# Two-layer transformer sandwich, fp32: in the attention steps the value matmuls go ahead of all the step's row-maximum scores

## The chip, the core and the metric

One Trainium2 chip; the kernel runs on one of its cores. The metric is device time of one execution in microseconds (us). The kernel before takes 1508.69 us, the median of three executions (1508.69 to 1511.38).

Names in the profile: PE is TensorE (matmuls), PEld its weight loads, DVE is VectorE, ACT is ScalarE, POOL is GpSimd, SP is SyncE, which here only issues DMAs. "L725" is line 725 of the kernel. A group such as `ex<-psc,mask` names the tile written and the tiles read.

## The reference

Activations `x` are 2 batches x 1024 tokens x 512, fp32. Four blocks, each of the form x = x + layernorm(block(layernorm(x))):

1. a grouped-query block in which each head's softmax runs over one score,
2. a feed-forward block with ternary weights (512 to 1408 to 512),
3. causal attention with rotary position embedding, 16 heads of width 32, 4 key/value groups (four heads to a group), 1024 tokens,
4. a feed-forward block (512 to 2048 to 512) with 2:4 sparsity of the hidden values.

The change lies in block 3, which computes

```
q = x @ q_w.T ; k, v = split(x @ kv_w.T)      # q, k rotated
logits = q @ k.T / sqrt(32) + causal mask
probs  = softmax(logits)
out    = (probs @ v) @ c_w.T
```

## The kernel before, in words

**Tiling of the attention.** A task is one batch, one block Q of 512 queries (two per batch) and one key/value group with its four heads: 2 x 2 x 4 = 16 tasks. Keys come in tiles of 128. With Q = 0 a task looks at 4 key tiles, with Q = 1 at 8.

**Scores are computed twice.** The softmax needs each row's maximum and sum first, and the probabilities with keys on the partitions afterwards.

- The *row-maximum scores* (`score_step`, tile `psc`, L725) have 128 queries on the partitions and up to 512 keys in the free dimension. For each PSUM tile DVE adds the mask, writes the negated scores to SBUF (`ex`) and takes the running minimum (L736); for Q = 1 a head's row has two such chunks, and the second takes the first's result (`mx`) as its start. Then ACT runs the exponential over the row with its sum (L742, `ex<-ex,mxs`).
- When a task's scores are done, some 20 small DVE instructions compute minus the logarithm of the sum plus the maximum (`minus_log`, L184, tiles `lg*`), split it into three bf16 pieces (`pm`), and PE transposes these (L955) to `mT`. The small DVE instructions are kept in a list and dropped, two after each score pass, into DVE's order (`drip`).
- The *key-side scores* (`prob_step`, tile `pst`, L1021) have 128 keys on the partitions and 512 queries in the free dimension, one matmul for each of the four heads; a bf16 *shift matmul* for each head (L1028) adds `mT` to them in PSUM. ACT then takes the exponential (L1034), which is the finished probability `pT`. On the diagonal POOL sets the masked part to zero (L1036), and tiles there are narrower: 512, 384, 256, 128.
- The *values* (`value_step`, tile `po`, L1050) multiply `pT` by `v`: eight matmul instructions (fp32 in two passes for four heads), 32 output columns each.

**Order.** PE and POOL run in the order in which the code issues them; DVE is so ordered only where the code says so (score passes and small drops), and otherwise DVE and ACT are ordered by the compiler's scheduler. The main loop (L1301) makes 96 steps, one for each key tile of each task. In step s: key-side scores and shifts of tile s, then row-maximum scores of a *later* task, then the values of tile s-1, whose exponentials have run meanwhile, then whatever is due in this step (projections `pq`, `pkv` of the next batch, output products `py` of a finished one, transposes). `wanted` (L1210) says how many row-maximum steps must be done by then, at a rate of 4/3 for each step, so a step has none, one (4 matmuls) or two (8).

The values are not put ahead of or behind all of these scores but after the first half of the first row-maximum step: `scores_up_to` calls `between` after the first group of heads, and `between` runs the values once. If a step has no scores, the values come directly after the shifts.

**PSUM.** Eight banks. Key-side scores and row-maximum scores share a ring of seven (`ring`: tags `a` with four and `o` with three, in turn), so each new tile needs the bank of the tile seven before it, emptied by ACT (`pst`) or DVE (`psc`). Values accumulate in the eighth (`ps_v`). `ex` has three buffers, `pT` four (two to a step).

```
L1198  for n_h, heads in enumerate(hs):
L1199      score_step(tk, ii, heads, ring)
L1200      if n_h == 0:
L1201          between()
...
L1307  waiting = [lambda: values(step)]
...
L1314  scores_up_to(wanted(step), step, between)
L1315  between()
```

Of the kernel before, what the change touches and what calls it, by code (L numbers as in the profile page):

```python
# [24 lines left out]
def two_layer_sandwich(  # L25
# [175 lines left out]
    def in_order(f):  # L201
        with tc.manual_schedule(engines={mybir.EngineType.DVE}):
            f()

    def drip(n, idle=False, upto=None):


        while n > 0 or (upto is not None and len(shift_drops.items) > upto):
            q = shift_drops if shift_drops.items else norm_drops
            if not q.items:  # L210
                return
            f, cost = q.items.pop(0)
            n -= cost
            if f is not None:
                f()
            elif idle:
                while q.items and q.items[0][0] is None:
                    q.items.pop(0)
                return
# [363 lines left out]
    def flush():  # L583
        while waiting_adds:
            waiting_adds.pop(0)()
# [121 lines left out]
    def score_sums(tk, pool):  # L707
        tk.mx = pool.tile([P, GT, REP], F32, tag="mxs", name=f"mxs_{tk.nm}", bufs=3)
        tk.sm = pool.tile([P, GT, REP], F32, tag="sms", name=f"sms_{tk.nm}", bufs=3)

    def score_step(tk, ii, heads, bank):


        n = GW * tk.Q + (ii + 1) * P
        for r in heads:
            ex = None
            if tk.n > 0:
                ex = s1.tile([P, NQ * GW], F32, tag="ex", name=f"ex_{tk.nm}_{ii}_{r}", bufs=3)
            mx = tk.mx[:, ii, r : r + 1]
            least = 3.0e38  # L720
            for ch in range(tk.Q + 1):
                k0 = ch * GW
                w = min(GW, n - k0)
                pa = bank(f"psc_{tk.nm}_{ii}_{ch}_{r}")
                nc.tensor.matmul(  # L725
                    pa[:, :w], tk.q.bitcast(F32R)[:, r, ii * P : (ii + 1) * P],
                    tk.st.k[ch].bitcast(F32R)[:, tk.g, :w], start=True, stop=True,
                )
                to, m0 = mx, GW + P - w
                if ch < tk.Q:  # L730
                    to = s1.tile([P, 1], F32, tag="mx1", name=f"mx1_{tk.nm}_{ii}_{r}", bufs=4)
                    m0 = 0
                if tk.n == 0:
                    ex = pa
                with tc.manual_schedule(engines={mybir.EngineType.DVE}):
                    nc.vector.tensor_tensor_reduce(  # L736
                        out=ex[:, k0 : k0 + w], in0=pa[:, :w], in1=mask[:, m0 : m0 + w],
                        scale=-1.0, scalar=least, op0=ALU.add, op1=ALU.min, accum_out=to,
                    )
                    drip(2)  # L740
                least = to
            nc.scalar.activation(  # L742
                ex[:, :n], ex[:, :n], AF.Exp, scale=-1.0, bias=mx,
                accum_out=tk.sm[:, ii, r : r + 1],
            )

    with tc.manual_schedule(engines={mybir.EngineType.PE, mybir.EngineType.Pool}):
# [69 lines left out]
        for g in range(NG):  # L817
            nxt = None
            for hc in range(HC):
# [70 lines left out]
                step = HC * g + hc  # L890
# [123 lines left out]
    def prob_step(tk, j):  # L1014

        st, g = tk.st, tk.g
        jj = j - GT * tk.Q
        c0 = max(jj, 0) * P
        pas = [ring(f"pst_{tk.nm}_{j}_{r}") for r in range(REP)]
        for r in range(REP):  # L1020
            nc.tensor.matmul(  # L1021
                pas[r][:, c0:],
                st.k[j // GT].bitcast(F32R)[:, g, (j % GT) * P : (j % GT + 1) * P],
                tk.q.bitcast(F32R)[:, r, c0:], start=True, stop=False,
            )
        for r in range(REP):
            rows = slice(DK * r, DK * r + DK)
            nc.tensor.matmul(  # L1028
                pas[r][:, c0:], onesb[rows, :], tk.mT[rows, c0:], start=False, stop=True
            )  # L1030
        for pr in range(2):
            p = s1.tile([P, 2, GW], F32, tag="pT", name=f"pT_{tk.nm}_{j}_{pr}", bufs=4)
            for e in range(2):
                nc.scalar.activation(p[:, e, c0:], pas[2 * pr + e][:, c0:], AF.Exp)  # L1034
            if jj >= 0:
                nc.gpsimd.affine_select(  # L1036
                    out=p[:, :, c0 : c0 + P], in_=p[:, :, c0 : c0 + P],
                    compare_op=ALU.is_ge, fill=0.0, base=0,
                    pattern=[[0, 2], [1, P]], channel_multiplier=-1,
                )  # L1040
            tk.pT[j, pr] = p

    def value_step(tk, j):
        st, g = tk.st, tk.g
        c0 = max(j - GT * tk.Q, 0) * P
        last = GT * tk.Q + GT - 1
        if j == 0:
            tk.po = ps_v(f"po_{tk.nm}")
        for r in range(REP):
            nc.tensor.matmul(  # L1050
                tk.po[DK * r : DK * r + DK, c0:], st.v[j // GT][:, j % GT, g * DK : (g + 1) * DK],
                tk.pT[j, r // 2][:, r % 2, c0:], start=(j == 0), stop=(j == last),
            )
        del tk.pT[j, 0], tk.pT[j, 1]
        if j == last:
            if g == 0:
                st.oT[tk.Q] = s1.tile([P, NKV, GW], F32, tag="oT", name=f"oT_{tk.nm}", bufs=1)
            nc.vector.tensor_copy(st.oT[tk.Q][:, g, :], tk.po)
# [63 lines left out]
    def later(step, parts, apart=1):  # L1122
        for k, f in enumerate(parts):
            due.setdefault(step + k * apart, []).append(f)
# [35 lines left out]
    def load_upto(n):  # L1160

        while loaded[0] < min(n, len(tasks)):
            tk = tasks[loaded[0]]
            tk.st = batch(tk.b)
            if done.get(tk.b, 0) < GT * (tk.Q + 1):
                return
            if tk.g == 0:
                load_k(tk.st, tk.Q)
            load_q(tk)
            loaded[0] += 1  # L1170

    with tc.manual_schedule(engines={mybir.EngineType.PE, mybir.EngineType.Pool}):
# [5 lines left out]
        s_end, n = {}, 0  # L1178
# [6 lines left out]
        def scored(tk):  # L1185
            shifts(tk)
            later(first[tk.n] - (1 if tk.n < 4 else 2), [lambda: maxima_T(tk)])

        def scores_up_to(n, step, between=lambda: None):
            nonlocal pos  # L1190
            while pos < min(n, len(s_steps)):
                tk, ii, ch = s_steps[pos]
                if ii == 0 and ch == 0:
                    load_upto(tk.n + 2)
                    assert loaded[0] > tk.n
                    score_sums(tk, s1)
                hs = (range(0, 2), range(2, 4)) if tk.Q == 0 else (range(2 * ch, 2 * ch + 1), range(2 * ch + 1, 2 * ch + 2))
                for n_h, heads in enumerate(hs):  # L1198
                    score_step(tk, ii, heads, ring)  # L1199
                    if n_h == 0:  # L1200
                        between()  # L1201
                pos += 1
                if pos == s_end[tk.n]:
                    scored(tk)
# [5 lines left out]
        def wanted(step):  # L1210
            return max(
                math.ceil(
                    s_end[tk.n]
                    - RATE * max(0, first[tk.n] - min(5, 3 + tk.n // 2) - step)
                )
                for tk in tasks
            )
# [8 lines left out]
        finish(0, GT + 1)  # L1226
        bank[0] = ring
        scores_up_to(pos + 1, -1)
        parts[GT + 3][0]()
        scores_up_to(pos + 1, -1)  # L1230
        parts[GT + 3][1]()
        scores_up_to(pos + 1, -1)
# [60 lines left out]
        def values(step):  # L1293
            if len(prev) < 2 and step < len(t_steps):
                return
            ptk, pj = prev.pop(0)
            value_step(ptk, pj)
            if pj == GT * ptk.Q + GT - 1 and ptk.g == NKV - 1:
                later(step + 1, output_parts(ptk.st, ptk.Q))

        for step, (tk, j) in enumerate(t_steps):  # L1301
            hold_adds[0] = True
            prob_step(tk, j)
            flush()
            prev.append((tk, j))

            waiting = [lambda: values(step)]  # L1307

            def between():
                while waiting:  # L1310
                    waiting.pop()()

            before = pos
            scores_up_to(wanted(step), step, between)  # L1314
            between()  # L1315
            idle, upto = pos == before, 6 * max(0, ready[0] - step)
            in_order(lambda: drip(8 if idle else 2, idle, upto))
            for f in due.pop(step, []):
                f()
# [3 lines left out]
        while due:  # L1323
            step = min(due)
# [313 lines left out]
    with tc.manual_schedule(engines={E.PE, E.Activation, E.DVE, E.SP, E.Pool}):  # L1638
        for g in range(NG):
            more = g + 1 < NG  # L1640
            hs = []
# [112 lines left out]
```

## Time and profile before

| | |
|---|---|
| median of three executions | 1508.69 us |
| profiled execution, its own time | 1512.6 us |
| its span, first to last instruction | 1510.9 us |
| attention steps | 437 to 901 us of the span |
| granted TensorE clock, whole span / attention steps | 0.974 / 0.94 |
| DVE passes over row-maximum scores, 512 wide (L736, first or only chunk) | 156 in the steps, mean 687 ns |
| ACT exponential of a 1024-wide row (L742) | 32, mean 1156 ns, and 201 ns for its sum |
| ACT exponential of 512 key-side scores (L1034) | 192, mean 609 ns |
| POOL select on the diagonal (L1036) | 128, mean 415 ns |

All of these are rows of one profiled execution. Matmuls overlap in the array, so a matmul's own duration (0.4 to 0.6 us here) says less than the time from one start to the next. The idle time of an engine is put down to whoever released it last; idle time off the path that sets the end costs nothing. The chain that ended last is followed back from the end: at each step to what released the instruction, or to the one before it on its engine.

### The profile page before, as it was taken

How to read it: one execution, taken by the hardware profiler on the slowest of the kernel's cores; microseconds unless marked ns; L12 is line 12 of the kernel's file. 1: busy time of each engine (PE TensorE's matmuls, PEld its weight loads, DVE VectorE, ACT ScalarE, POOL GpSimd, SP SyncE). 2: the span in 40 equal slices, each digit the busy share in tenths (PEclk: the TensorE clock that was granted, in tenths of full speed). 3: DMA queues.
4: the chain of work that ended last, by engine and by line, in shares of the span. 5: the costliest groups of instructions: out<-in, count | busy, mean ns of one | idle time of the engine just before them, and what ended most of it. 6: DMA issues, size and time to landing. Idle time of an engine off the chain costs nothing.

```text
span 1510.9 us, 19884 instructions
## 1 busy us (share of the span) xinstructions
PE 1436.6 (95%) x6742; PEld 1031.1 (68%) x6742; DVE 1016.8 (67%) x2666; ACT 704.9 (47%) x1583; POOL 320.6 (21%) x425
## 2 busy tenths in 40 slices
PE   7999999999888899998999999999999999999997
PEld 4558888767645454434444447888888888888886
DVE  6976464752477767757778735884688468846773
ACT  4242343322467655798786963450344044404420
POOL 1104475432222314323432011000200010011001
PEclk9999999999989999999899999999999999999998
DMA  8200211201365243344342005523452355236312
GB/s 299 77 14 28 84 57 43 52 18 36 90 183 139 91 129 91 100 132 98 98 112 98 2 1 192 198 98 146 174 195 98 147 190 207 90 137 218 141 49 77
DMA packets 78869, 167.36 MB, mean 111 GB/s; under 512 B 10224, under 2 KB 35824, under 8 KB 76720
## 3 DMA queue, kind: packets, MB, share of 16 engines
q1 hardware_dynamic: 72928, 148.26, 30.0%
q0 software_dynamic: 4784, 16.52, 2.9%
q10 hardware_dynamic: 1056, 1.31, 0.2%
q8 instruction: 53, 0.87, 0.2%
q14 instruction: 48, 0.39, 0.1%
HBM read 138.81 MB, written 27.26 MB: 110 GB/s over the span
## 4 chain that ended last, share of the span: by engine, by line
PE 81%; DVE 8%; ACT 7%; issue 2%; POOL 2%; DMA 1%; SPq 0%; DVEq 0%; ACTq 0%; POOLq 0%
PE acc L1514 13%; PE ph L428 9%; PE pb_u L1363 7%; PE pb_g L1363 7%; PE po L447 4%; PE pst L1021 4%; PE py L1093 4%; PE pq L622 4%; ACT ex L742 4%; PE pc_u L1363 4%; PE pc_g L1363 4%; PE pq L305 4%; PE psc L725 3%; PE po L1050 3%; ACT pT L1034 2%; DVE ex L736 2%
## 5 line engine op out<-in xcount | busy, mean ns | idle before, releaser
L742 ACT ACTIVATE ex<-ex,mxs 128x640 f32<-128x640 f32 (+7 forms) x240 | 188.3, 794 | 37.6 <-DVE mxs L736 30.8
L1034 ACT ACTIVATE pT<-pst 128x512 f32<-128x512 f32 (+3 forms) x384 | 158.4, 501 | 77.4 <-PE pst L1028 77.1
L428 PE MATMUL ph<-xTg,w 128*128 128x512 f32 x704 | 173.5, 400 | 1.7 <-DVE xTg L418 0.9
L736 DVE CUSTOM_DVE_ANT_0 ex<-psc,mask 128x512 f32<-128x512 f32 (+3 forms) x240 | 139.8, 593 | 43.8 <-PE psc L725 32.0
L428 PEld LDWEIGHTS ph<-xTg,w 128*128 128x128 f32 x704 | 133.3, 191 | 31.8 <-DVE xTg L418 1.2
L1567 POOL TENSOR_TENSOR x_sb<-x_sb,o 128x512 f32<-128x512 f32 x14 | 19.1, 1362 | 549.4 <-DVE o L256 549.3
L1514 PE MATMUL acc<-wd,h 128*128 128x256 f32 x512 | 121.6, 379 | 0.0
L1036 POOL TENSOR_SCALAR_AFFINE_SELECT pT<-pT 128x256 f32<-128x256 f32 x128 | 52.4, 415 | 297.5 <-ACT pT L1034 295.5
L1514 PEld LDWEIGHTS acc<-wd,h 128*128 128x128 f32 x512 | 97.0, 190 | 13.1
L1050 PE MATMUL po<-pT,v 128*32 128x512 f32 (+3 forms) x768 | 92.5, 521 | 2.3 <-POOL pT L1036 2.2
L1514 PE MATMUL acc<-wd,hx 128*128 128x256 f32 x384 | 93.3, 379 | 0.0
L437 POOL TENSOR_TENSOR hl<-h,hl 128x512 fp32r<-128x512 f32 x44 | 57.1, 1302 | 161.2 <-ACT hl L436 161.1
L447 PE MATMUL po<-w,hl 128*128 128x512 f32 x352 | 88.0, 392 | 0.4 <-DVE tmp L256 0.3
L434 DVE TENSOR_TENSOR h<-h,ph 128x512 f32<-128x512 f32 x44 | 30.0, 684 | 85.6 <-PE ph L428 75.5
L1514 PEld LDWEIGHTS acc<-wd,hx 128*128 128x128 f32 x384 | 73.0, 190 | 9.9
L1424 DVE TENSOR_TENSOR gate<-gate,ab 128x1024 f32<-128x1024 f32 x32 | 39.2, 1225 | 59.2 <-ACT ab L1421 59.2
L447 PEld LDWEIGHTS po<-w,hl 128*128 128x128 f32 x352 | 65.8, 188 | 15.5 <-DVE tmp L256 1.3
L1531 ACT COPY p<-acc 128x512 f32<-128x512 f32 x8 | 4.7, 584 | 152.2 <-PE acc L1514 152.2
L736 DVE CUSTOM_DVE_ANT_0 ex<-psc,mask,mx 128x128 f32<-128x128 f32 (+3 forms) x128 | 69.1, 547 | 7.3 <-PE psc L725 0.4
L436 ACT CAST hl<-h 128x512 fp32r<-128x512 f32 x44 | 27.3, 620 | 85.9 <-DVE h L434 85.9
L1021 PE MATMUL pst<-q,k 128*128 128x512 f32 (+3 forms) x192 | 57.3, 401 | 10.1 <-ACT pT L1034 5.5
L725 PE MATMUL psc<-k,q 128*128 128x512 f32 (+3 forms) x192 | 61.9, 387 | 4.5 <-DVE mxs L736 2.5
(304 smaller groups left out, 3065.8 us busy)
## 6 DMA issues: line engine op xcount, KB each, us to landing
w<-kept SPq DMA_DIRECT2D x64, 512.0 KB, 5.9
wd<-keptd SPq DMA_DIRECT2D x16, 1024.0 KB, 8.3
q<-dq SPq DMA_DIRECT2D x48, 256.0 KB, 5.0
w<-in_f_wg SPq DMA_DIRECT2D x32, 384.0 KB, 3.3
w<-in_f_wu SPq DMA_DIRECT2D x32, 384.0 KB, 5.4
wd<-in_f_wd SPq DMA_DIRECT2D x16, 768.0 KB, 5.4
dq<-hl SPq DMA_DIRECT2D x32, 320.0 KB, 3.1
kept<-wl POOLq DMA_DIRECT2D x16, 512.0 KB, 3.0
```

The costliest lines, as they stand in the source:

```text
L305: nc.tensor.matmul(pa[:, :n], xT[:, c, :], w[:, c, :], start=(c == 0), stop=False)
L428: nc.tensor.matmul(pa, wt[:, c, cols], xT[:, s, c, :], start=(c == 0 and s == 0), stop=(c == DC - 1 and s == 1),)
L447: nc.tensor.matmul(pos0[g][k], hl[:, s, k * P : (k + 1) * P], w3[:, hc, :], start=(hc == 0 and s == 0), stop=(hc == HC - 1 and s == 1),)
L622: nc.tensor.matmul(pq, h.xT[:, c, :], wq1[:, c, :], start=(c == 0), stop=(c == DC - 1))
L725: nc.tensor.matmul(pa[:, :w], tk.q.bitcast(F32R)[:, r, ii * P : (ii + 1) * P], tk.st.k[ch].bitcast(F32R)[:, tk.g, :w], start=True, stop=True,)
L736: nc.vector.tensor_tensor_reduce(out=ex[:, k0 : k0 + w], in0=pa[:, :w], in1=mask[:, m0 : m0 + w], scale=-1.0, scalar=least, op0=ALU.add, o ...
L742: nc.scalar.activation(ex[:, :n], ex[:, :n], AF.Exp, scale=-1.0, bias=mx, accum_out=tk.sm[:, ii, r : r + 1],)
L1021: nc.tensor.matmul(pas[r][:, c0:], st.k[j // GT].bitcast(F32R)[:, g, (j % GT) * P : (j % GT + 1) * P], tk.q.bitcast(F32R)[:, r, c0:], star ...
L1034: nc.scalar.activation(p[:, e, c0:], pas[2 * pr + e][:, c0:], AF.Exp)
L1050: nc.tensor.matmul(tk.po[DK * r : DK * r + DK, c0:], st.v[j // GT][:, j % GT, g * DK : (g + 1) * DK], tk.pT[j, r // 2][:, r % 2, c0:], sta ...
L1363: nc.tensor.matmul(p, a[:, c, :], b[:, c, :], start=(first and c == 0), stop=(c == 1), skip_group_check=not first,)
L1514: nc.tensor.matmul(acc[m // 2][:, m % 2 * HW : (m % 2 + 1) * HW], a[:, j, k * P : (k + 1) * P], b[:, j, :], start=start, stop=True, skip_g ...
```

## The change

The values of tile s-1 are issued straight after the shift matmuls of tile s, ahead of all row-maximum scores of the step. The scores then come in one row: four or eight matmuls without the values between them. `between` and its list go away. Nothing else is edited; no instruction is added or removed.

```diff
-        def scores_up_to(n, step, between=lambda: None):
+        def scores_up_to(n, step):
...
-                for n_h, heads in enumerate(hs):
+                for heads in hs:
                     score_step(tk, ii, heads, ring)
-                    if n_h == 0:
-                        between()
...
-            waiting = [lambda: values(step)]
-
-            def between():
-                while waiting:
-                    waiting.pop()()
-
+            values(step)
             before = pos
-            scores_up_to(wanted(step), step, between)
-            between()
+            scores_up_to(wanted(step), step)
```

## The prediction

> **What bounds the kernel now.** First the busy shares of the page, then the busy times of the attention stage alone (437 to 901 us, where all the moved instructions lie), then who waits for whom there, then single steps of the timeline and of the chain that ended last.
>
> ```profile
> PE 1436.6 (95%) x6742; PEld 1031.1 (68%) x6742; DVE 1016.8 (67%) x2666; ACT 704.9 (47%) x1583; POOL 320.6 (21%) x425
> ```
>
> ```profile
> 437.00:901.00 464.00, 426.77 (x2272) 211.96 (x2273) 335.43 (x1245) 347.09 (x868) 137.66 (x237) 0.94 0.34 95
> ```
>
> The columns of the second are stretch, length, busy time (and instructions) of PE, PEld, DVE, ACT and POOL, granted clock, DMA share, GB/s. Over the span PE bounds. In the stage PE is busy 92%, but DVE has 335 and ACT 347 of 464 us, and a busy PE row there holds late matmuls too, so PE is not simply the limit. The waits of the stage (total, times, longest):
>
> ```profile
> DVE ex L736 <- PE psc L725: 32.1, 41, 2.0
> ACT ex L742 <- DVE mxs L736: 30.0, 45, 2.6
> PEld pst L1021 <- DVE mxs L736: 16.1, 31, 1.4
> PEld pst L1021 <- ACT pT L1034: 15.8, 32, 1.7
> PEld psc L725 <- ACT pT L1034: 14.1, 28, 2.5
> PEld po L1050 <- POOL pT L1036: 9.6, 17, 1.5
> ```
>
> So the three engines wait for each other round a ring of seven PSUM banks: PE for banks that DVE and ACT must empty, DVE for scores, ACT for maxima. Which wait ends last differs from step to step. Two steps, first one in which nothing is late (PE rows alone):
>
> ```profile
> 612.34 0.39 PE L1028 MATMUL pst<-mT,onesb 32*128 32x512 bf16 x4
> 612.66 0.50 PE L725 MATMUL psc<-qk,q 128*128 128x512 f32 x1
> 613.00 0.39 PE L725 MATMUL psc<-k,q 128*128 128x512 f32 x1
> 613.31 1.07 PE L1050 MATMUL po<-pT,v 128*32 128x512 f32 x8
> 614.31 0.50 PE L725 MATMUL psc<-qk,q 128*128 128x512 f32 x1
> 614.64 0.40 PE L725 MATMUL psc<-k,q 128*128 128x512 f32 x1
> 614.88 1.09 PE L1021 MATMUL pst<-q,k 128*128 128x512 f32 x4
> ```
>
> Start to start: first score pair 0.65, values 1.00, second pair 0.57 us; inside, 0.34 and 0.31, then 0.33 and 0.24. Now one in which DVE is waiting for the first scores:
>
> ```profile
> 518.31 0.51 PE L725 MATMUL psc<-qk,q 128*128 128x512 f32 x1
> 518.80 0.85 PE L1050 MATMUL po<-pT,v 128*32 128x384 f32 x8
> 518.85 0.69 DVE L736 CUSTOM_DVE_ANT_0 ex<-psc,mask 128x512 f32<-128x512 f32 x1 [1.71 <-PE psc L725]
> 519.59 0.50 PE L725 MATMUL psc<-qk,q 128*128 128x512 f32 x1
> ```
>
> DVE had stood idle 1.71 us, and its work on the first pair runs beside the values. The chain that ended last shows which of the two kinds counts. It runs straight down PE at 612, and leaves PE for DVE at 518, to come back to PE only at 526.3:
>
> ```profile
> 612.73 0.65 PE psc L725 x2
> 613.38 0.99 PE po L1050 x8
> 614.38 0.66 PE psc L725 x2
> ```
>
> ```profile
> 518.38 0.45 PE psc L725
> 518.83 0.02 issue
> 518.85 0.69 DVE ex L736
> ```
>
> **The change.** Nothing is added or removed. In the built programs the PE order differs in 65 of the 96 attention steps: in each, two score matmuls (130 in all) stand behind the step's eight value matmuls instead of ahead of them. POOL's 392 and SP's 260 rows keep their order, so no DMA is moved past anything. Bank numbers keep too, as values use a bank of their own. What is queued behind the values on PE is now the whole row of scores, so every first pair comes later by the length of the values: 0.36, 0.57, 0.78 or 1.00 us by width (V below).
>
> *One change of matmul shape less.* In the free step, a row of four scores would take 0.34 + 3 x 0.24 = 1.06 instead of 0.65 + 0.57 = 1.22: 0.16 us saved. The chain passes from first pair to values on PE in 30 of the 65 steps: 30 x 0.16 = -4.8 us. In the other 35 PE waits later in the step anyway: 0.
>
> The Trainium skill (TensorEngine Tiling (Array Packing), Key Properties) has it that a change of the tiling mode drains the engine, and the order before has four such changes a step, the new one three. The rule speaks for the change. Taken alone it would give all 65 steps their 0.16, 10.4 us, and the sum below would be -0.9; the chain says that over half of the steps do not have PE on their path, so the row of 30 stands.
>
> *First pairs that are late themselves.* In nine of those 30 the first pair waits for a bank, and the values wait behind it although their inputs are there: 463.9 us (pair 1.13, free 0.66), 501.8 (3.14, 0.66), 631.6 (0.92, 0.55), 635.7 (1.89, 0.55), 689.8 (1.19, 0.66), 736.1 (1.44, 0.55), 772.9, 823.5 and 848.7 (0.92 to 0.93, 0.55 to 0.61). Values first fill that wait, up to their own length: 0.47 + 0.57 + 0.37 + 0.36 + 0.53 + 0.89 + 0.37 + 0.32 + 0.37 = 4.25. All of it is gained if the second pair's banks come no later than it does; nothing if they do. Neither is nearer: half, -2.1 (0 to -4.2).
>
> *DVE starved on the chain.* Where the chain leaves PE from the first pair to DVE, DVE starts V later, and all behind it. Places 451.6, 492.8 (the chain names ACT in between, but DVE starts 0.66 us after the pair's first matmul, as at 612, where it is 0.64), 518.3, 597.3, 741.6, 809.5 us: 0.78 + 1.00 + 0.78 + 1.00 + 0.36 + 0.78 = 4.7. At 472.6, 627.3, 768.2 and 844.4 the chain goes to DVE just after the values; its backlog there begins with the first pair, so it is late by V less the idle that DVE has now between the two pairs (0, 0.23, 0.11, 0.23): 0.78 + 0.55 + 0.67 + 0.55 = 2.55. Together +7.2. Most of these are steps with eight scores, after which the next step's fourth key-side matmul needs the bank of the fifth score: there is what is late next.
>
> *First pair to ACT.* At 454.9, 541.2, 779.8 and 857.0 the chain goes from first pair to ACT's exponentials. If these need the pair, V each, 3.6 us; if ACT works from its backlog (it is idle under 0.3 us in each of these steps), 0. Half: +1.8.
>
> *DVE's own order.* With four scores at hand at once, the built program lets DVE take the next head's first chunk before this head's second in 54 places, 21 before. In 33 more places a head's maximum comes one 512-wide pass later, 0.69 us. ACT waited for a maximum 45 times in 231: 33 x 45/231 x 0.69 = 4.4 at most, 0 if backlog covers it; half, +2.2.
>
> *Values earlier.* They now start when the shifts end. Against the ends of POOL's selects, that is too early in one of the 65 steps, at 681.3 us, by 0.8 at most; half, +0.4.
>
> *Costed at nothing.* In 19 more steps DVE stands idle before the first pair, V summing to 13.9 us. In a four-score step the first bank is wanted again only by the next step's fourth key-side matmul: at 612 the pair would be at DVE at 614.3, done at 615.0, wanted at 615.7, so 0.6 us of cover. From 640 to 657 and from 827 to 841 ACT never stops, and its exponentials start over 1 us after their maximum (651.3 to 653.0). If these covers fail, up to 13.9.
>
> Sum: -4.8 - 2.1 + 7.2 + 1.8 + 2.2 + 0.4 = +4.7 us. The profiled execution took 1512.6 (span 1510.9, 1.7 around it) and would take 1517.3. It stands 3.9 above the median of the runs; on 1508.7 the same sum gives 1513.4.
>
> **Rivals.** About 0.2%, 3 us, is what a measurement can tell from no change.
>
> *Faster.* DVE idles 129 us of the stage, and where it starts late it may catch up before PE asks for the bank; then both gains stand in full (-9.0) against some 3 for what is left of the rest: -6, 1502.7. For it: the first-pair waits of 14.1 us on ACT. Against: from the starved places the chain stays on DVE for up to 7.4 us (518.9 to 526.3). It decides once the starved places and the three small terms cost under 6.0 of their 7.2 + 4.4.
>
> *No change.* Gains and losses are of like size, and every term but the first can come out near zero: 1505.7 to 1511.7.
>
> *Much slower.* The cover of the 19 other steps fails, since DVE's row of scores is in one block and its swapped order gives banks back late: the key-side matmuls, already waiting for DVE 16.1 us, wait 13.9 more, 1527. Against: the 0.6 us of cover at 612.
>
> *The order is not what it says:* excluded by the 130 moved matmuls.
>
> **How the numbers follow.** Likeliest is slower by a few us: 1513.4, own range 1511.7 to 1520, chance 0.45. Much slower 0.13, no change 0.21, faster 0.21. So slower 0.58, same 0.21, faster 0.21. The range leaves out the deepest part of faster (all gains in full, -9 us) and the end where all bounds add (+25): 1503 to 1527.
>
> **What would show it.** Right: DVE's wait for scores rises from 32.1 by ten or more, ACT's wait for maxima above 30.0, the key-side matmuls' wait for DVE rises, the score matmuls' wait for ACT falls from 14.1; span outside 437 to 901 unchanged. Wrong: the stage shrinks, or the key-side waits stay where they are while DVE waits more, which would mean that DVE's idle was never on the path. Longer waits of the values for POOL, above 12 us, would mean that the selects were hidden by the first pair.

## The result, and the profile after

The kernel with the change takes 1522.91 us (median of four executions, 1521.46 to 1526.26); the kernel before, on the same chip, 1510.04. The ratio is 1.0084, with a 95% interval from 1.0058 to 1.0110: slower by about 12.7 us. The forecast was 1513.4 in a range of 1503 to 1527, and slower. Sign and range hold, but the sum (+4.7) was less than half of what came, and the time lies above the range of the likeliest case alone (1511.7 to 1520).

The profiled execution took 1521.46 us (span 1519.8). Its attention steps begin 1.9 us earlier than in the profile before, and from the last step's start to the end both profiles take 613.3 us, so the loss lies in the steps. From the first step's start to the last step's start it was 458.4 us before and is 469.2 now: +10.8.

The busy shares, then the busy times of the attention stage, now 437 to 912 us (stretch, length, PE, PEld, DVE, ACT, POOL, granted clock, DMA share, GB/s):

```profile
PE 1427.9 (94%) x6742; PEld 1032.6 (68%) x6742; DVE 1009.7 (66%) x2666; ACT 704.2 (46%) x1583; POOL 320.8 (21%) x425
```

```profile
437.00:912.00 475.00, 419.82 (x2273) 214.95 (x2272) 328.05 (x1239) 344.68 (x862) 136.94 (x236) 0.94 0.33 93
```

The clock is the same 0.94, the work is the same, and every engine is idle for longer. The waits of the stage (total, times, longest):

```profile
DVE ex L736 <- PE psc L725: 56.1, 43, 4.5
ACT ex L742 <- DVE mxs L736: 40.2, 38, 2.2
PEld psc L725 <- ACT pT L1034: 21.8, 34, 1.5
PEld pst L1021 <- ACT pT L1034: 20.7, 25, 2.1
PEld pst L1021 <- DVE mxs L736: 15.5, 31, 1.4
PEld po L1050 <- POOL pT L1036: 9.7, 19, 0.8
```

DVE's wait for scores rose by 24.0 us and ACT's wait for maxima by 10.2, as foretold. The other end of the ring did not behave as foretold: the key-side matmuls' wait for DVE stayed (16.1 before), and the score matmuls' wait for ACT rose from 14.1 instead of falling.

The step in which nothing is late, PE rows alone:

```profile
608.94 1.06 PE L1050 MATMUL po<-pT,v 128*32 128x512 f32 x8
609.93 0.50 PE L725 MATMUL psc<-qk,q 128*128 128x512 f32 x1
610.27 0.40 PE L725 MATMUL psc<-k,q 128*128 128x512 f32 x1
610.50 0.39 PE L725 MATMUL psc<-qk,q 128*128 128x512 f32 x1
610.73 0.39 PE L725 MATMUL psc<-k,q 128*128 128x512 f32 x1
610.96 0.62 PE L1021 MATMUL pst<-q,k 128*128 128x512 f32 x2
```

Four scores take 610.96 - 609.93 = 1.03 us, where two pairs took 0.65 + 0.57 = 1.22: 0.19 us saved. And the step in which DVE had waited for the first score, from the timeline (DVE's row says that it was idle for 2.63 us ahead of it, 1.71 before the change) and from the chain that ended last:

```profile
513.85 1.28 PE L1050 MATMUL po<-pT,v 128*32 128x384 f32 x8
...
514.29 0.14 PEld L1050 LDWEIGHTS po<-pT,v 128*32 128x32 f32 x4 [0.30 <-POOL pT L1036]
...
515.06 0.50 PE L725 MATMUL psc<-qk,q 128*128 128x512 f32 x1
...
515.60 0.69 DVE L736 CUSTOM_DVE_ANT_0 ex<-psc,mask 128x512 f32<-128x512 f32 x1 [2.63 <-PE psc L725]
```

```profile
515.13 0.44 PE psc L725
515.57 0.02 issue
515.60 0.69 DVE ex L736
...
523.07 0.47 PE pst L1021
```

As before the change, the chain leaves PE at the first score and comes back to PE 7.5 us later. This step became 1.20 us longer. Of these, 0.78 are the values' length; the other 0.43 come from the values themselves, which now start before their inputs are done: the second four wait for POOL's select (the row at 514.29), so the eight take 1.21 us from start to start instead of 0.78.

Comparing the two profiles step by step (a step's length is taken from its first key-side matmul to that of the next step) tells which steps lose:

| steps | number | sum of the changes in length |
|---|---|---|
| with eight scores | 22 | +13.1 us |
| with four scores | 44 | -2.5 us |
| without scores | 29 | +0.3 us |

(The sums are rounded; they add to +10.8. The last step is left out, as its end is not marked in the same way.) The loss is in the steps with eight scores, 21 of the 65 in which scores were moved.

### The profile page after: what moved, and what is told of

The parts are those of the page before. It is cut to its first block, busy times and chain, and to the rows that moved or that the text cites. A ratio compares the mean times of both kernels' runs of the same rounds, so it can differ in the third digit from the quotient of the medians.

```text
span 1519.8 us, 19858 instructions
## 1 busy us (share of the span) xinstructions
PE 1427.9 (94%) x6742; PEld 1032.6 (68%) x6742; DVE 1009.7 (66%) x2666; ACT 704.2 (46%) x1583; POOL 320.8 (21%) x425
## 4 chain that ended last, share of the span: by engine, by line
PE 80%; DVE 9%; ACT 7%; issue 2%; POOL 2%; DMA 0%; DVEq 0%; SPq 0%; ACTq 0%; POOLq 0%
PE acc L1506 13%; PE ph L428 9%; PE pb_u L1355 7%; PE pb_g L1355 7%; PE po L447 4%; PE po L1050 4%; ACT ex L742 4%; PE pq L305 4%; PE pq L622 4%; PE pc_g L1355 4%; PE pc_u L1355 4%; PE py L1093 4%; PE pst L1021 3%; PE psc L725 3%; DVE ex L736 3%
## 5 line engine op out<-in xcount | busy, mean ns | idle before, releaser
L742 ACT ACTIVATE ex<-ex,mxs 128x640 f32<-128x640 f32 (+7 forms) x240 | 187.3, 789 | 48.3 <-DVE mxs L736 41.1
L736 DVE CUSTOM_DVE_ANT_0 ex<-psc,mask 128x512 f32<-128x512 f32 (+3 forms) x240 | 136.6, 592 | 68.5 <-PE psc L725 56.6
L1506 PEld LDWEIGHTS acc<-wd,h 128*128 128x128 f32 x512 | 97.0, 190 | 13.1
L1021 PE MATMUL pst<-q,k 128*128 128x512 f32 (+3 forms) x192 | 56.9, 397 | 14.5 <-ACT pT L1034 10.3
L736 DVE CUSTOM_DVE_ANT_0 ex<-psc,mask,mx 128x128 f32<-128x128 f32 (+3 forms) x128 | 66.5, 545 | 0.2
L1355 PE MATMUL pb_u<-xdg,w 128*128 128x256 f32 x256 | 65.8, 379 | 0.0
```

Source lines behind the costliest of these rows:

```text
L736: nc.vector.tensor_tensor_reduce(out=ex[:, k0 : k0 + w], in0=pa[:, :w], in1=mask[:, m0 : m0 + w], scale=-1.0, scalar=least, op0=ALU.add, o ...
L742: nc.scalar.activation(ex[:, :n], ex[:, :n], AF.Exp, scale=-1.0, bias=mx, accum_out=tk.sm[:, ii, r : r + 1],)
L1021: nc.tensor.matmul(pas[r][:, c0:], st.k[j // GT].bitcast(F32R)[:, g, (j % GT) * P : (j % GT + 1) * P], tk.q.bitcast(F32R)[:, r, c0:], star ...
L1355: nc.tensor.matmul(p, a[:, c, :], b[:, c, :], start=(first and c == 0), stop=(c == 1), skip_group_check=not first,)
L1506: nc.tensor.matmul(acc[m // 2][:, m % 2 * HW : (m % 2 + 1) * HW], a[:, j, k * P : (k + 1) * P], b[:, j, :], start=start, stop=True, skip_g ...
```

## Experiments

Each kernel was timed in five rounds against the kernel before on the same chip; the ratio is to that. Most of them use one small generalisation: the place of the values is counted in groups of scores (two matmuls each) ahead of them, apart for steps with four and with eight scores.

```diff
         def scores_up_to(n, step, between=lambda: None):
             nonlocal pos
+            groups = 2 * max(0, min(n, len(s_steps)) - pos)
+            at, n_h = {2: A4, 4: A8}.get(groups, 1), 0
...
-                for n_h, heads in enumerate(hs):
+                for heads in hs:
+                    if n_h == at:
+                        between()
                     score_step(tk, ii, heads, ring)
-                    if n_h == 0:
-                        between()
+                    n_h += 1
```

With A4 = A8 = 1 this is the order before, with A4 = A8 = 0 that of the change.

### Which steps lose: four scores or eight

```diff
+            at, n_h = {2: 0, 4: 1}.get(groups, 1), 0
```

> Values ahead of the scores only in the 44 steps with four scores; in the 22 steps with eight the values stay behind the first pair. Theory R (row of eight): the eighth score of a row needs the bank of the row's first score, so a row of eight started behind the values makes PE wait for DVE's first pass inside the row; four-score steps do not have that and keep the free step's gain of about 0.2 us. It expects this kernel 2 to 8 us faster than the kernel before (the four-score steps of the change sum to -2.5 us in its profile, their 23 gains alone to -14.4, but part of these only make up for a late step ahead of them). The prediction's own terms, split by step: 23 x -0.16, late first pairs -2.0, starved +1.1, half the swapped order +1.1: -3.4 us. Theory S (DVE's swapped order costs the time, and most of the swaps stay: 44 of 54 in the built program, 21 before): 23 of 33 extra swaps remain, so some 0.7 of the loss, +7 us or more against the kernel before.

Measured: 1511.62 against 1511.60, ratio 1.0001 (0.9991 to 1.0011). No change: neither R's gain of 2 us or more nor the prediction's -3.4 came, and S is out.

```diff
+            at, n_h = {2: 1, 4: 0}.get(groups, 1), 0
```

> The complement: values ahead only in the 22 steps with eight scores, behind the first pair in the 44 with four. Theory R: it carries the whole loss, +11 to +16 us against the kernel before, more than the change itself (+12.9). The prediction's terms, split: seven changes of shape less -1.1, late pair -0.2, starved places +6.1, first pair to ACT +1.8, half the swapped order +1.1, earlier values +0.4: +8.1 us. Theory S (30 swaps in the built program, 21 before, 54 with the whole change): 9 of 33 extra swaps, so some 0.3 of the loss, about +3.5 us.

Measured: 1523.03 against 1511.60, ratio 1.0079 (1.0065 to 1.0092), +11.9 us. The 22 steps with eight scores carry the whole loss. In this kernel's profile they are 11.7 us longer than before, and the row of scores itself accounts for 10.1 of it. The stretch of the values accounts for 2.2 (over the stage they wait 22 times for POOL's selects, 17 times before); the rest of these steps is somewhat shorter.

The waits of these two runs say something more. DVE's wait for scores in the kernel with four-score steps alone, then in that with eight-score steps alone:

```profile
DVE ex L736 <- PE psc L725: 43.6, 45, 2.2
```

```profile
DVE ex L736 <- PE psc L725: 46.6, 45, 2.8
```

Against 32.1 before, DVE stands idle 11.5 us more in the one and 14.5 us more in the other. The first costs nothing, the second 12 us. How long an engine waits does not tell what its wait is worth.

Here is one step with eight scores (widths 512 and 128 for each of four heads), first in the kernel before, then with the values ahead (PE's and DVE's rows):

```profile
844.42 0.56 PE L725 MATMUL psc<-k,q 128*128 128x512 f32 x2
844.91 0.85 PE L1050 MATMUL po<-pT,v 128*32 128x384 f32 x8
844.96 0.69 DVE L736 CUSTOM_DVE_ANT_0 ex<-psc,mask 128x512 f32<-128x512 f32 x1 [0.84 <-PE psc L725]
...
845.69 1.25 PE L725 MATMUL psc<-k,q 128*128 128x512 f32 x6
845.80 0.35 DVE L736 CUSTOM_DVE_ANT_0 ex<-psc,mask,mx 128x128 f32<-128x128 f32 x1
...
846.78 0.40 PE L955 MATMUL pmt<-identb,pm 128*128 128x128 bf16 x4
```

```profile
853.45 0.85 PE L1050 MATMUL po<-pT,v 128*32 128x384 f32 x8
854.23 1.62 PE L725 MATMUL psc<-k,q 128*128 128x512 f32 x8
854.77 0.69 DVE L736 CUSTOM_DVE_ANT_0 ex<-psc,mask 128x512 f32<-128x512 f32 x1 [1.62 <-PE psc L725]
...
855.38 0.69 DVE L736 CUSTOM_DVE_ANT_0 ex<-psc,mask 128x512 f32<-128x512 f32 x1
...
855.99 0.35 DVE L736 CUSTOM_DVE_ANT_0 ex<-psc,mask,mx 128x128 f32<-128x128 f32 x1
...
856.40 0.38 PE L955 MATMUL pmt<-identb,pm 128*128 128x128 bf16 x4 [0.55 <-DVE mxs L736]
```

The next tile after the row, that of the transposes (L955), takes here the bank of the row's second score, seven tiles earlier. Before, DVE's pass over the first score began at 844.96, beside the values, and the second score was done well before PE asked for its bank at 846.78. Now DVE begins 0.78 us later, counted from the shifts, takes the two first chunks ahead of the second ones, and PE stands 0.55 us. The step goes from 3.46 to 4.04 us.

Which tile held a bank before can be read from the built programs, and it is not always the tile seven places earlier, as the rule of the ring would have it. Of the 736 score tiles of the steps, of both kinds, 480 take the bank of the seventh tile before them in the kernel before; for the others it is a tile two to fifteen places back. With the change, 163 of the 736 follow another tile in their bank than before. In all 22 rows of eight the first score's bank is asked for again inside the row: with the change by the eighth score in 15 of them, by the fifth or sixth in seven. The new distribution of the banks does not carry the loss. The kernel with the values ahead in four-score steps alone differs in 135 tiles and loses nothing; the one with them ahead in eight-score steps alone differs in 67 and loses as much as the change.

An eighth score that stands for the first one's bank, in the profile of the change (PE's rows and one of DVE's):

```profile
715.68 1.07 PE L725 MATMUL psc<-k,q 128*128 128x128 f32 x7
...
717.41 0.28 DVE L736 CUSTOM_DVE_ANT_0 ex<-psc,mask 128x128 f32<-128x128 f32 x1
...
717.75 0.39 PE L725 MATMUL psc<-k,q 128*128 128x256 f32 x1 [1.00 <-DVE mxs L736]
718.05 3.70 PE L1093 MATMUL py<-wc,oT 128*128 128x512 f32 x8
```

Seven scores in a row, 1.00 us of waiting, the eighth, and only then the output products. In this step DVE was not idle ahead of the row: it was busy from 714.04 on with small logarithm instructions and an output copy, and began its first pass 1.73 us after the first score had begun (1.03 before the change). So PE stands in the row whether DVE comes late from idling or from other work.

### DVE's swapped order

The row of the change, with DVE held to PE's order:

```diff
-                for n_h, heads in enumerate(hs):
-                    score_step(tk, ii, heads, ring)
-                    if n_h == 0:
-                        between()
+                with tc.manual_schedule(engines={mybir.EngineType.DVE}):
+                    for heads in hs:
+                        if n_h == at:
+                            between()
+                        score_step(tk, ii, heads, ring)
+                        n_h += 1
```

(with A4 = A8 = 0)

> The whole change, but DVE's passes over the scores of a row are held in the order in which PE writes them (17 places out of order in the built program; 54 with the change, 21 before). Theory S: most of the loss goes, the time comes within 4 us of the kernel before. Prediction's term: 2.2 us back (0 to 4.4), so +8.5 to +13 against the kernel before. Theory R: the first pass of a row is not made earlier by that, so the loss stays: +10 to +14.

Measured: 1522.19 against 1511.60, ratio 1.0070 (1.0057 to 1.0084), +10.6 us. Passes out of order fell from 54 to 17 and most of the loss stayed, so the swaps are not its cause. Between this and the change lie some 2 us, the size of the prediction's term, but the two intervals overlap.

### Is it the late start, or the unbroken row

```diff
+            at, n_h = {2: 1, 4: 4}.get(groups, 1), 0
```

> The kernel before, but in the 22 steps with eight scores the values stand behind all eight, not behind the first pair: the row is unbroken as in the change, and DVE gets its first pair as early as before. Theory D (DVE paces the row: its eight passes take longer than PE's eight scores, so the start of its first pass sets when the row's banks come back, and the values' length is lost in nearly every step with eight scores): DVE starts as early as before, so little is lost, -4 to +4 us against the kernel before. Theory U (an unbroken row: eight scores without the values among them run into banks that ACT and DVE have not emptied, wherever the row stands): as slow as the change, +8 to +13 us.

Measured: 1508.71 against 1510.82, ratio 0.9985 (0.9974 to 0.9996), -2.3 us. The same unbroken row of eight, begun early and with the values behind it, does not lose but gains slightly. U's number is out. In the profile the time is moved: steps with eight scores are 13.7 us longer in sum, as PE runs into banks inside the row, and the steps with four scores 15.8 shorter. That fits DVE and ACT being less behind after such a row: ACT's wait for maxima (L742 for L736) goes from 30.0 to 21.7 us.

Two kernels test whether DVE's passes set the pace. Both use half passes; ACT keeps the length of its exponentials (1178 ns for 1024 elements, 1156 before), DVE's pass over 512 falls from 0.69 to 0.42 us:

```diff
-                        out=ex[:, k0 : k0 + w], in0=pa[:, :w], in1=mask[:, m0 : m0 + w],
+                        out=ex[:, k0 // d : (k0 + w) // d], in0=pa[:, : w // d], in1=mask[:, m0 : m0 + w // d],
...
+                src = ex[:, : n // 2].unsqueeze(1).to_broadcast([P, 2, n // 2])
+                dst = ex[:, n // 2 : n].bitcast(BF16).rearrange("p (e t) -> p e t", e=2)
```

> The order of the kernel before; DVE's pass over the row-maximum scores takes only the first half of each chunk, and ACT's exponential runs twice over that half, so it keeps its length (the maximum and the sum are those of half of the keys; only DVE's pass gets shorter: 0.42 instead of 0.69 us for a 512-wide chunk, by the 256-wide passes of the trace). It is the base for the next kernel. 384 passes lose some 0.2 us of DVE each; faster than the kernel before by 5 to 25 us under either theory.

Measured: 1493.37 against 1510.82, ratio 0.9885 (0.9866 to 0.9903), -17.4 us: DVE's passes are on the path.

> As the kernel with half passes, and the values ahead of the scores in the 22 steps with eight scores. The difference to the half-pass kernel counts; with whole passes it is +12 us (1523.0 against 1511.6). Theory D: with DVE's eight passes down from some 4.2 to 2.8 us it no longer paces the row, and the difference falls to +4 us or less. Theory U: ACT's work and PE's row are as before, the difference stays at +8 to +13 us.

Measured: 1500.75, ratio 0.9926 (0.9910 to 0.9942). Against the half-pass kernel it is +7.4 us by the medians, and by the two ratios 0.0041, 6.2 us, with some 3.7 either way if their errors are independent. Neither side's number came: more than D's 4, less than U's 8. The profiles divide it. Steps with eight scores are 4.0 us longer with half passes, where they were 11.7 longer with whole ones; the rows of scores in them 2.1 instead of 10.1. So DVE's pace is the cause of most of the loss inside the row. The same step as above, with half passes and the values ahead:

```profile
835.83 0.85 PE L1055 MATMUL po<-pT,v 128*32 128x384 f32 x8
836.61 1.60 PE L726 MATMUL psc<-k,q 128*128 128x512 f32 x8
837.14 0.42 DVE L737 CUSTOM_DVE_ANT_0 ex<-psc,mask 128x256 f32<-128x256 f32 x1 [1.63 <-PE psc L726]
...
838.18 0.40 PE L960 MATMUL pmt<-identb,pm 128*128 128x128 bf16 x4
```

DVE begins as late, but PE does not stand ahead of the transposes, and the step takes 3.45 us, as it does with half passes and the values behind the first pair (3.46). Some 3.6 us more are lost in the other steps, four-score steps and steps without scores. What passes it on there was not tested; ACT, whose exponentials wait for the late maxima (18.5 us with half passes, 24.8 with the values ahead as well), is the candidate.

### No rows of eight

```diff
-        RATE = 4.0 / 3.0
+        RATE = 1.0
```

with the order of the change.

> The whole change, and scores are made at the rate of one score step for each attention step instead of 4/3: 84 steps with four scores, none with eight. Against the kernel before it mixes two things (its pair, the same rate with the values behind the first pair, is to be run next). Theory R: with no row of eight the values-first order loses nothing, and the 84 free steps gain up to 0.2 each; expected -10 to +3 us against the kernel before. The prediction's starved places (DVE starts later by the values' length wherever the chain leaves PE for DVE) do not need a row of eight; by it this kernel stays slower than the kernel before by 5 us or more.

Measured: 1539.67 against 1511.60, ratio 1.0187 (1.0169 to 1.0205), +28 us. This rate puts twelve score steps, three tasks, ahead of the first attention step, and there are two buffers for the shift pieces (`pm`): the third task's pieces overwrite the first one's before they are transposed, so some softmax shifts are another task's. In the profile the steps begin at 456.7 us instead of 437 to 439, four score steps and a wait of 8.3 us of the transposes for the pieces later, and take 468.4 us, about as long as with the change (469.2), without one row of eight. Theory R's number is missed. The same rate with the values behind the first pair was not run, so this run does not tell what the order is worth without rows of eight; it does tell that spreading the scores in this way is no way round the loss.

### Beginning even earlier

```diff
+            if groups == 4:          # the first pair, then the key side
+                score_step(tk, ii, hs[0], ring)
+            keys()                   # prob_step(...), as before
+            values(step)
```

(The order is shown, not the text of the edit, which passes `prob_step` to `scores_up_to` as a second function like `between`.)

> The kernel before, but in the steps with eight scores the first pair stands ahead of the key-side scores, one to two us earlier; then key side, shifts, values and six scores. Theory D: DVE's first pass starts earlier by up to the length of the key side, where DVE stood idle; faster than the kernel before, -10 to -2 us. Theory U: the values still stand behind the first pair, nothing changes in the row: -2 to +3 us. The prediction has no term for it, but by its starved places (six of them in steps with eight scores, 6.1 us) it would be some 3 to 6 us faster.

Measured: 1517.86 against 1510.82, ratio 1.0042 (1.0029 to 1.0055). The loads of the next task's queries, which a task's first score step issues, were moved ahead of the key side with the pair; in one step the key-side scores waited for them:

```profile
465.72 1.09 PE L1021 MATMUL pst<-qk 128*128 128x128 f32 x4 [11.07 <-DMA qk<-dq]
```

With the loads left behind the key side:

```diff
+                        load_upto(to_load)      # behind keys()
```

> Again the first pair ahead of the key side in the 22 steps with eight scores, but where such a step opens a task, the loads of the next task's queries stay behind the key side (ahead of it they overwrote the queries that this step's key-side scores still need, so the run before computed some tiles with another task's queries, and PE stood 12 us for a load in one step). Theory D (DVE paces the row of eight; the sooner its first pass starts, the better): without that 12 us stall the run before would have ended some 5 to 8 us ahead of the kernel before, so -8 to -2 us. Rival, key side first (the pair ahead delays the key-side scores by 0.4 to 0.65 us, ACT's probabilities start later, and ACT has little slack): 0 to +6 us.

Measured: 1511.29 against 1513.16, ratio 0.9983 (0.9974 to 0.9992), -2.6 us, at the small end of what D expects. The 11.07 us of that one wait are more than the 6.3 us which the run before had lost.

### Can the parts be added

```diff
+            at, n_h = {2: 0, 4: 4}.get(groups, 1), 0
```

> Values ahead of the scores in steps with four, behind all of them in steps with eight. By the two separate runs (1511.62 against 1511.60, and 1508.71 against 1510.82) the effects add to -2 us. Theory D has nothing against it: DVE's first pass of a row of eight starts early, and four-score steps pay nothing for the values ahead. If the gain of values behind the eight scores came from the four-score steps after it, which ran 15.8 us shorter in sum while the eight-score steps ran 13.7 longer, values ahead there take some of it back: 0 to +4 us.

Measured: 1517.73 against 1513.16, ratio 1.0034 (1.0022 to 1.0047), +5.1 us.

```diff
+            at, n_h = {2: 2, 4: 4}.get(groups, 1), 0
```

> The opposite of the change: values behind all row-maximum scores in every step that has any, four or eight. Theory D: DVE's passes begin as early as the key side lets them, the values have slack; at least as good as values behind all eight alone (-2.1 us against the kernel before): -6 to 0 us. Against it: in a step with four scores nothing was gained or lost by the values' place ahead (+0.0), so none may be lost or gained behind: then -3 to -1 us. If the values do not have the slack (the last of them frees the PSUM tile that DVE copies out, and the output products follow), 0 to +6 us.

Measured: 1515.71 against 1511.45, ratio 1.0029 (1.0019 to 1.0040), +4.4 us.

The first pair ahead of the key side in steps with eight scores, and the values behind all eight:

```diff
-            (at_k, at), n_h = {2: (0, 1), 4: (1, 1)}.get(groups, (0, 1)), 0
+            (at_k, at), n_h = {2: (0, 1), 4: (1, 4)}.get(groups, (0, 1)), 0
```

> In steps with eight scores: the first pair ahead of the key side (loads kept behind it), then key side, shifts, six scores, values; steps with four as in the kernel before. The two parts alone gave -2.2 us (0.9983) and -2.1 us (0.9985). If they gain in different ways they add: -4 us. If both only give DVE's first passes and their banks time ahead of PE, as theory D has it, the second adds little: -3 to -1 us.

Measured: 1512.70 against 1511.45, ratio 1.0006 (0.9997 to 1.0014).

None of the three adds up. The first two lose where theory D expected a gain, and the third gains nothing. With values behind the eight scores, a step with four scores may have its values neither ahead (+5.1) nor behind (+4.4), though with the rest as before their place ahead cost nothing. The waits of the kernel with all values last say what happens at that end:

```profile
PEld psc L725 <- ACT pT L1034: 39.0, 66, 2.0
DVE ex L736 <- PE psc L725: 30.3, 39, 2.6
ACT ex L742 <- DVE mxs L736: 25.7, 33, 2.7
```

DVE and ACT wait less than in the kernel before, but the score matmuls wait 39.0 us for ACT (14.1 before): in 31 of the 44 four-score steps of this program the fourth score wants the bank of the step's first key-side tile, which ACT still has to empty, and the values no longer stand in that gap. So theory D holds for the late start of a row of eight, and is not the whole account: by these waits, the values also fill PE's wait for ACT.

The best two kernels, values behind all eight scores (0.9985) and the first pair ahead of the key side (0.9983), are about 2 us faster than the kernel before, and so faster than the change.

## Why the prediction was right or wrong

**The sign and the mechanism were right.** DVE, begun late by the values' length, returns banks and maxima late. The ten starved places were to cost 7.2 us; their steps became 6.1 us longer in sum. The four places where the first pair goes to ACT were to cost 1.8 (0 to 3.6); 2.9. The nine late first pairs were to gain 2.1; their steps are 2.5 shorter.

**The step that failed is "costed at nothing".** It gave 19 more steps with an idle DVE no cost, by a cover of 0.6 us read off the step at 612, which has four scores. Three of the 19 have eight scores and lost 1.5 us (+1.20, +0.34, 0); the 16 with four scores became 1.0 longer. Four more steps with eight scores, in which DVE was busy right up to its first pass, have no term at all and lost 2.7 us (+1.10, +1.14, +1.11, -0.62). What the cover overlooked is who asks first. In a row of eight the first score's bank is asked for inside the same step, by the eighth score or an earlier one, and the second's often by the tile after the row; the prediction looked for the next asker in the next step. So 18 of the 22 steps with eight scores are longer, and all 22 together by 13.1 us, where the free lengths of their values add to 17.7.

Two premises of that cover do not hold in the built programs. The banks did not keep: although values have a bank of their own, only 207 of the 736 score tiles of the steps have the same bank number before and after the change. And in a four-score step the first bank is wanted by the next step's fourth key-side matmul in six of 44 cases of the kernel before, in 26 by an earlier key-side matmul of that step, in 12 by a tile of the same step. The four-score steps lost nothing end to end even so.

**Values earlier was too small.** At 681.3 us +0.4 was said, and the step lost 1.2, nearly all of it in the values. They were too early in three more steps, all with eight scores, which begin at 513.0, 663.1 and 811.2 us in the profile of the change: there the values take 0.38 to 0.43 us longer than before.

**The gains did not reach the end.** A change of shape less was sized well, even low, for steps like the one it was read from: 0.19 to 0.20 us in the seven steps in which nothing is late and the scores are 512 wide, against 0.16. In four other steps without a wait, with narrower scores and values 128 wide, it was only 0.06 to 0.08. The Trainium skill, TensorEngine Tiling (Array Packing), Key Properties, says that a change of the tiling mode drains the engine; these savings fit that, though no row shows the drain itself. By an estimate with 0.2 us for all 65 steps, the gain would have been some 13 us. But already the 4.8 us from 30 steps of the chain were too much. Split by step, the prediction had -3.4 us for the steps with four scores, and the run with the change in these alone gave 0.0 (-1.4 to +1.7). In its profile the four-score steps are 4.2 us shorter, and the others 5.5 longer: what PE gains in the one kind of step comes back as length in the other. All the steps that are in none of these groups changed by -1.2 together; -4.8 + 2.2 was to come from changes of shape and from DVE's own order, but 15 of the 30 steps behind the -4.8 are in the groups above, so this line is not a clean check of either term.

In sum, over the 95 steps of the profiles: -2.5 (late pairs) + 6.1 (starved) + 2.9 (to ACT) + 1.2 (681.3) + 4.3 (seven steps with eight scores, 1.5 costed at nothing and 2.7 without a term) - 1.2 (the rest) = +10.8, where -2.1 + 7.2 + 1.8 + 0.4 + 0 - 2.6 = +4.7 was foretold. These are differences of step lengths in one profile each, and a step can be longer for what an earlier one did.

**The observables.** DVE's and ACT's waits rose as said, POOL's stayed under 12 us, the rest of the span was unchanged. The key-side matmuls' wait for DVE did not rise; PE is now stopped inside the row, before it comes to them. The prediction would have taken that, with DVE waiting more, as a sign that DVE's idle was never on the path, and that reading was wrong. The score matmuls' wait for ACT rose instead of falling.

**The rivals.** *Much slower* named the failing cover and put it at the next step's key-side matmuls; the cover did fail, in the steps with eight scores alone and inside the row. *Faster* and *No change* are out for the change as a whole; *No change* is what the steps with four scores do by themselves.

## What to carry to other kernels

In a ring of buffers, look for each length of a row who asks first for the bank of the row's first element, and look in the built program, as the banks need not go round in turn: with seven banks a row of eight asks for it within itself, and a cover read off a shorter row doesn't hold. What stands ahead of such a row delays the slower engine that empties the banks by its whole length, while the same work among it, or behind it in these rows alone, cost nothing here. A rise in an engine's wait is no price: 11.5 us of it were worth nothing in one kind of step and 14.5 us were worth 12 us in the other, and gains measured apart here did not add.

## What the runs showed of the hardware

- A row of four 128x512 scores without other shapes among them took 1.02 to 1.04 us in seven steps without a wait, against 1.22 to 1.24 in two pairs round values 384 or 512 wide: 0.19 to 0.20 us for one change of matmul shape and back. With narrower scores (four of 384, or 512 and 256 in turn) round values 128 wide it was 0.06 to 0.08 us.
- Half of the elements made this DVE pass over PSUM shorter, but not by half: 0.69 us for 512, 0.42 for 256, 0.28 for 128.
- ACT's exponential read from half as many elements twice and written as bf16 took as long as the plain one: 1178 against 1156 ns for 1024 elements.
- The attention steps began between 437.1 and 440.2 us in eight profiled executions whose order on PE is the same up to there. That scatter is as large as the smallest effects here, which only repeated rounds could tell from nothing.
